# A PSUM source for VectorE's pair differences, and a second of four tiles for GpSimd

## The chip, the cores and the metric

The kernel runs on one core of a Trainium2 chip. A core has TensorE (PE in the profile, with its weight loads as PEld), VectorE (DVE), ScalarE (ACT), GpSimd (POOL), and queues that issue DMAs (SP's above all). The metric is device time of one execution in microseconds (us); lower is better.

## The reference, cut to what matters

Four graph layers, each `x = x + layer(relu(layernorm(x)), adj)`, over 128 graphs of 128 nodes with 128 channels, all in float32. Layer 1 is the one that the change touches:

```python
D = jnp.abs(x[:, :, None, :] - x[:, None, :, :])      # 128 graphs x 128 x 128 pairs x 128 channels
h = jnp.einsum('bijc,oc->bijo', D, W1) + b1           # 64 outputs for each pair
m = jnp.mean(h, axis=(0, 1, 2))                       # a batch norm over all pairs of all graphs
v = jnp.mean((h - m) ** 2, axis=(0, 1, 2))
h = _leaky((h - m) / jnp.sqrt(v + EPS) * g1 + be1)
s = jnp.einsum('bijo,uo->biju', h, W2)[..., 0] + b2[0]   # then mask, softmax, A @ x, Wg, batch norm, Wt
```

Layer 0 sums, for 7 relations r, the neighbours with `adj == r` through a weight of their own, normalizes and adds. Layers 2 and 3 are masked attention.

## The kernel before, in words

The work goes in 32 groups of G = 4 graphs, and in three stages, since each batch norm of layer 1 needs a sum over all graphs first.

Stage one (lines 216 to 311) holds layer 0 and the pairs of layer 1. `layer0(g)` loads a group, normalizes (`pre_norm`, lines 156 to 165: L146 and L148 statistics on DVE, `rsqrt` on POOL at L140 and L141, L153 scale and L164 relu on DVE), transposes (L170 on PE, L171 on ACT), and for each graph builds a mask tile of 7 relations on DVE (L253), multiplies by the relation weights on PE (`ph`, L259), copies to SBUF on ACT (`hw`, L261), multiplies by the masks on PE (`pa`, L265, and the degrees, L268), and adds the parts up on DVE (L274). Then it normalizes the sum `o` (L279 to L285), stores `x`, normalizes again (`hn`, L290) and transposes into `xe` (L294), an SBUF tile with the channels on the partitions and the first 64 of the 128 nodes repeated at the end (L297, on POOL).

`pairs(g)` takes the pairs (i, j) of one graph by distance: 64 distances in four tiles t = 0 to 3, each of 2 halves x 8 distances x 128 nodes = 2048 elements on 128 partitions. For one tile, `pairwise` (lines 177 to 193) does this:

- `d = xe[shifted] - xe` (L185), one instruction with two SBUF inputs, on POOL where t is in `ON_POOL`, else on DVE;
- the absolute value in place on ACT (L187);
- four matmuls with W1 into a PSUM tile of two banks (`hp`, L191).

`pair_stats` then copies `hp` to SBUF on ACT (`hs`, L205), takes its statistics on DVE (L206, L208, L210) and, once a graph, stores `hs` in HBM (L211).

`_weave` (line 39) writes the program so that four steps of `layer0(g + 2)` follow each tile of `pairs(g)`. A scheduler in the compiler then orders each engine's instructions by its own estimates of durations; each engine runs its order strictly from front to back. So in each group the program has a mixed stretch, in which the matmuls of layer 0 alternate with those of some eight tiles, and a plain stretch of the remaining tiles, in which only the two norms at the end of layer 0 and the first norm of the next group's layer 0 go along. Buffers that set the order: three of `d` (the tag "d"), two of `hp` (the PSUM tag "big", 4 of 8 banks), four of the PSUM tag "sm" (the other 4 banks: `pt`, `po`, `ph`, `pa` in stage one, and nearly all small products later), three of `xe`.

Stage two (line 316 to the `behind` loop) reads the stored `hp` back, applies the batch norm and W2, and does layer 1's softmax and sums. Stage three (`group`, line 576) does the end of layer 1 and layers 2 and 3. Both take their PSUM tiles from the tags "sm" and "big".

Of the kernel before, what the change touches and what calls it, by code (L numbers as in the profile page):

```python
# [9 lines left out]
F32 = mybir.dt.float32  # L10
# [6 lines left out]
P = 128  # L17
G = 4
# [7 lines left out]
KH = 32  # L26
KC = 8
ROW = P + 2 * KH
ON_POOL = {1}
AHEAD = 2  # L30
NT = KH // KC

# [26 lines left out]
def tile_gnn_stack(ctx: ExitStack, tc: tile.TileContext, a: dict, out: bass.AP):  # L59
    nc = tc.nc  # L60
# [6 lines left out]
    psum = ctx.enter_context(tc.tile_pool(name="psum", bufs=1, space=bass.MemoryType.PSUM))  # L67
# [2 lines left out]
        return psum.tile([P, 2, 512], F32, tag="big", bufs=2, name=name)  # L70

    def sm(name):
        return psum.tile([P, G, P], F32, tag="sm", bufs=4, name=name)


    ident = const.tile([P, P], F32, name="ident")
# [51 lines left out]
    HT = [dr.tile([P, G, P], F32, tag=f"h{g}", name=f"h{g}") for g in range(NG)]  # L128
# [24 lines left out]
            nc.vector.tensor_scalar(dst[:, k, :], src[:, k, :], mv[:, k, 0:1], rs[:, k:k + 1],  # L153
                                    op0=OP.subtract, op1=OP.mult)

    def pre_norm(pool, src, mv=None, rs=None):

        if mv is None:
            mv = small.tile([P, G, 2], F32, name="lnmv")
            rs = small.tile([P, G], F32, name="lnrs")  # L160
            norm_stats(src, mv, rs)
        h = pool.tile([P, G, P], F32, tag="hn", name="hn")
        norm(h, src, mv, rs)
        nc.vector.tensor_scalar(h, h, 0.0, None, op0=OP.max)  # L164
        return h

    def transpose(dst, src):
        pt = sm("pt")
        for k in range(G):
            nc.tensor.transpose(pt[:, k, :], src[:, k, :], ident)  # L170
        nc.scalar.copy(dst, pt)  # L171
# [2 lines left out]
        return t[:, None, :].to_broadcast([P, G, P])  # L174


    def pairwise(pool, xe, k, t):

        d = pool.tile([P, 2, KC, P], F32, tag="d", bufs=3, name="d")
        x = xe[:, k, 0:P]  # L180
        ahead = xe[:, k, 1 + KC * t:]
        ahead = bass.AP(tensor=ahead.tensor, offset=ahead.offset,
                        ap=[list(ahead.ap[0]), [KH, 2], [1, KC], [1, P]])
        eng = nc.gpsimd if t in ON_POOL else nc.vector
        eng.tensor_tensor(d, ahead, x[:, None, None, :].to_broadcast([P, 2, KC, P]), OP.subtract)  # L185
        d = d.rearrange("p h k i -> p h (k i)")
        nc.scalar.activation(d, d, AF.Abs)  # L187
        hp = big("hp").rearrange("p a b -> p (a b)")
        for c in range(0, KC * P, 512):
            for hh in range(2):  # L190
                nc.tensor.matmul(hp[64 * hh:64 * hh + 64, c:c + 512], w1T, d[:, hh, c:c + 512],  # L191
                                 start=True, stop=True)
        return hp

    hsp = ctx.enter_context(tc.tile_pool(name="hsp", bufs=3))

    def pair_stats(pool, xe, k, b):


        st = small.tile([P, 9, 6], F32, name="st")  # L200
        hs = hsp.tile([P, NT, KC * P], F32, name="hs")
        for t in range(NT):
            yield
            hp = pairwise(pool, xe, k, t)
            nc.scalar.copy(hs[:, t, :], hp)  # L205
            nc.vector.bn_stats(st[:, 2 * t, :], hs[:, t, 0:512])  # L206
            last = t == NT - 1
            nc.vector.bn_stats(st[:, 2 * t + 1, :], hs[:, t, 512:1024 - P * last])  # L208
            if last:
                nc.vector.bn_stats(st[:, 8, :], hs[:, t, 1024 - P:])  # L210
        nc.sync.dma_start(HP[b], hs)  # L211
        nc.vector.bn_aggr(ST1[:, b, 0, :], st.rearrange("p a b -> p (a b)"))
        nc.vector.bn_aggr(ST1[:, b, 1, :], st[:, 8, :])


    with tc.tile_pool(name="c0", bufs=1) as c0, tc.tile_pool(name="p0", bufs=2) as p0:
        relw = load("relw", [P, 7, P], a["rel_w"][1:8].rearrange("r c d -> c r d"), pool=c0)
        selfwT = load("selfwT", [P, P], a["self_wT"], pool=c0)
        selfb = load("selfb", [P, P], _bcast(a["self_b"], P), pool=c0)
        gamma = load("gamma", [P, P], _bcast(a["gamma"], P), pool=c0)  # L220
        beta = load("beta", [P, P], _bcast(a["beta"], P), pool=c0)

        rel = c0.tile([P, 7], F32, name="rel")
        for r in range(7):
            nc.gpsimd.memset(rel[:, r:r + 1], float(r + 1))

        def layer0(g):
            bs = slice(g * G, g * G + G)
            hT = p0.tile([P, G, P], F32, name="hT")
            x = p0.tile([P, G, P], F32, name="x")  # L230
            nc.sync.dma_start(x, a["x"][bs].rearrange("b t c -> t b c"))
            adj = p0.tile([P, G, P], I32, name="adj")
            nc.sync.dma_start(adj, a["adj"][bs].rearrange("b t s -> t b s"))
            yield
            h = pre_norm(p0, x)
            yield
            adjf = p0.tile([P, G, P], F32, name="adjf")
            nc.vector.tensor_copy(adjf, adj)
            nc.gpsimd.tensor_scalar(M8[g], adjf, 0.0, None, op0=OP.is_gt)
            transpose(hT, h)  # L240
            yield
            adjT = p0.tile([P, G, P], F32, name="adjT")
            transpose(adjT, adjf)
            yield
            o = p0.tile([P, G, P], F32, name="o")
            po = sm("po")
            for k in range(G):
                nc.tensor.matmul(po[:, k, :], hT[:, k, :], selfwT, start=True, stop=True)
            nc.vector.tensor_tensor(o, po, over_group(selfb), OP.add)
            yield  # L250
            for k in range(G):
                mask = p0.tile([P, 7, P], F32, name="mask")
                nc.vector.tensor_tensor(mask, adjT[:, None, k, :].to_broadcast([P, 7, P]),  # L253
                                        rel[:, :, None].to_broadcast([P, 7, P]), OP.is_equal)

                for r0, r1 in ((0, 3), (3, 7)):
                    yield
                    ph = sm("ph")
                    nc.tensor.matmul(ph[:, 0:r1 - r0, :], hT[:, k, :], relw[:, r0:r1, :], start=True, stop=True)  # L259
                    hw = p0.tile([P, G, P], F32, name="hw", bufs=2)  # L260
                    nc.scalar.copy(hw[:, 0:r1 - r0, :], ph[:, 0:r1 - r0, :])  # L261
                    yield
                    pa = sm("pa")
                    for r in range(r0, r1):
                        nc.tensor.matmul(pa[:, r - r0, :], mask[:, r, :], hw[:, r - r0, :], start=True, stop=True)  # L265
                    if r0 == 0:
                        for r in range(7):
                            nc.tensor.matmul(pa[:, 3, r:r + 1], mask[:, r, :], ones[:, 0:1], start=True, stop=True)  # L268
                        rdeg = small.tile([P, 7], F32, name="rdeg")
                        nc.vector.tensor_scalar(rdeg, pa[:, 3, 0:7], 1e-6, None, op0=OP.max)  # L270
                        nc.vector.reciprocal(rdeg, rdeg)
                    yield
                    for r in range(r0, r1):
                        nc.vector.scalar_tensor_tensor(o[:, k, :], pa[:, r - r0, :], rdeg[:, r:r + 1],  # L274
                                                       o[:, k, :], op0=OP.mult, op1=OP.add)
            yield
            mv = small.tile([P, G, 2], F32, name="lnmv")
            rs = small.tile([P, G], F32, name="lnrs")
            norm_stats(o, mv, rs)  # L279
            yield  # L280
            norm(o, o, mv, rs)
            nc.vector.tensor_tensor(o, o, over_group(gamma), OP.mult)
            yield
            nc.vector.tensor_tensor(o, o, over_group(beta), OP.add)
            nc.vector.scalar_tensor_tensor(x, o, 0.0, x, op0=OP.max, op1=OP.add)  # L285
            nc.sync.dma_start(X[g], x)
            yield
            norm_stats(x, MV1[:, g], RS1[:, g])
            yield
            h = pre_norm(p0, x, MV1[:, g], RS1[:, g])  # L290
            yield

            xe = p0.tile([P, G, P + 2 * KH], F32, name="xe", bufs=AHEAD + 1)
            transpose(xe[:, :, 0:P], h)  # L294
            nc.sync.dma_start(HT[g], xe[:, :, 0:P])
            yield
            nc.gpsimd.tensor_copy(xe[:, :, P:], xe[:, :, 0:2 * KH])  # L297
            XE[g] = xe

        def pairs(g):  # L300
            xe = XE.pop(g)
            for k in range(G):
                yield from pair_stats(p0, xe, k, g * G + k)


        XE = {}
        for g in range(AHEAD):
            for _ in layer0(g):
                pass
        for g in range(NG):  # L310
            _weave(pairs(g), layer0(g + AHEAD) if g + AHEAD < NG else iter(()), 4)
# [359 lines left out]
```

## Time and profile before

| What | Value |
|---|---|
| median of 3 runs | 5709.03 us (5699.23 to 5712.11) |
| the profiled execution's own time | 5692.13 us |
| its span in the profile | 5690.3 us |
| stage one, of the span | to about 3010 us |
| stage two, of the span | about 3060 to 4400 us |
| stage three, of the span | about 4400 to 5690 us |
| busy in the span | PE 3734.1, DVE 3804.0, ACT 2626.8, POOL 816.0 us |

The profile is one execution. A row of its groups names line, engine, operation, output tile, input tiles and shape, the number of instructions, busy time in us, the mean duration of one in ns, and the idle time ahead of them with what ended it. PE runs at a granted share of its clock, which is given by stretches. The chain of waits follows, from the last instruction back, what released each step. Stage one repeats itself from group to group: the start of POOL's tile comes back every 90.8 us, for group after group.

### The profile page before, as it was taken

Reading aid. Unit: us, or ns where it says so; the run is one execution under the profiler, and the core shown is the slowest. Engines: PE = TensorE matmul, PEld = TensorE weight load, DVE = VectorE, ACT = ScalarE, POOL = GpSimd, SP = SyncE. Lnnn points to the kernel's source line nnn. Section 1 sums busy time; section 2 is a strip of 40 time slices with the busy share of each in tenths; the row PEclk is TensorE's granted clock in tenths of the full one; section 3 lists DMA queues with packets and bytes.
Section 4 is the critical chain, followed back from the end, with each engine's and each line's share of the span. In section 5 each row is a group of like instructions: output and inputs, shape, how many; then the busy total and the mean of one; then the engine's idle time right before and its main releaser. Section 6 shows DMA issues by size and latency. Waiting matters only on the chain.

```text
span 5690.3 us, 49171 instructions
## 1 busy us (share of the span) xinstructions
PE 3734.1 (66%) x17414; PEld 2055.7 (36%) x17414; DVE 3804.0 (67%) x7803; ACT 2626.8 (46%) x2434; POOL 816.0 (14%) x530
## 2 busy tenths in 40 slices
PE   5776767676777767676755555555546666666665
PEld 3332323232333323232312223322325555555554
DVE  6788888888888888888884333333336666665666
ACT  2455555555555555555565454444432222222222
POOL 2222222222222222222220000000000000000000
PEclk8888888888888888888876677667677667666676
DMA  1222222222222222222226666667640000000000
GB/s 48 100 100 104 96 104 96 118 98 102 98 102 113 102 104 96 104 96 109 98 113 270 260 259 253 244 255 272 242 179 14 15 8 15 11 12 15 8 15 10
DMA packets 167251, 634.40 MB, mean 111 GB/s; under 512 B 28512, under 2 KB 113760, under 8 KB 134240
## 3 DMA queue, kind: packets, MB, share of 16 engines
q1 hardware_dynamic: 150112, 622.87, 28.2%
q10 hardware_dynamic: 16896, 8.39, 0.5%
q8 instruction: 140, 2.29, 0.2%
q14 instruction: 103, 0.84, 0.0%
HBM read 324.18 MB, written 307.04 MB: 111 GB/s over the span
## 4 chain that ended last, share of the span: by engine, by line
PE 47%; DVE 28%; DMA 8%; ACT 7%; POOL 6%; issue 3%; SPq 0%; POOLq 0%; ACTq 0%; DVEq 0%
PE hp L191 15%; DVE d L185 6%; DMA rows<-sk 5%; ACT d L187 4%; PE ps L395 4%; PE pa L265 4%; PE ph L259 4%; PE pv L549 4%; PE pa L268 3%; DMA u<-rows 3%; POOL d L185 3%; PE pk L402 3%; PE pt L170 3%; DVE hn L153 2%; DVE st L206 2%
## 5 line engine op out<-in xcount | busy, mean ns | idle before, releaser
L191 PE MATMUL hp<-d,w1T 128*64 128x512 f32 x4096 | 1329.5, 742 | 798.1 <-ACT d L187 798.1
L187 ACT ACTIVATE d<-d 128x2048 f32<-128x2048 f32 x512 | 974.6, 1911 | 430.2 <-POOL d L185 224.6
L185 DVE TENSOR_TENSOR d<-xe 128x2048 f32<-128x2048 f32 x384 | 1099.6, 2863 | 14.0 <-PE hp L191 14.0
L191 PEld LDWEIGHTS hp<-d,w1T 128*64 128x64 f32 x4096 | 329.6, 164 | 1588.7 <-ACT d L187 951.6
L205 ACT COPY hs<-hp 128x1024 f32<-128x1024 f32 x512 | 516.0, 1008 | 515.6 <-PE hp L191 513.3
L185 POOL TENSOR_TENSOR d<-xe 128x2048 f32<-128x2048 f32 x128 | 544.4, 4253 | 1452.7 <-PE hp L191 1452.6
L391 ACT ACTIVATE z<-z,bias,scale 128x2048 f32<-128x2048 f32 x256 | 524.9, 2086 | 267.2 <-DMA z<-hp 267.1
L206 DVE BATCH_NORM_STATS2 st<-hs 128x6 f32<-128x512 f32 x512 | 350.8, 685 | 99.5 <-ACT hs L205 95.1
L170 PE MATMUL pt<-ident,e 128*128 128x128 f32 x768 | 154.9, 352 | 313.9 <-ACT e L533 233.0
L395 PE MATMUL ps<-z,w2z 128*32 128x512 f32 x2048 | 340.2, 782 | 4.7 <-ACT z L391 4.6
L265 PEld LDWEIGHTS pa<-hw,mask 128*128 128x128 f32 x1792 | 238.6, 205 | 252.3 <-issue 144.1
L208 DVE BATCH_NORM_STATS2 st<-hs 128x6 f32<-128x512 f32 (+1 forms) x512 | 329.0, 643 | 0.0
L430 PE MATMUL put<-ident,u 128*128 128x128 f32 x128 | 35.6, 434 | 437.8 <-DVE u L426 437.8
L265 PE MATMUL pa<-hw,mask 128*128 128x128 f32 x1792 | 289.6, 306 | 28.8 <-ACT hw L261 24.0
L261 ACT COPY hw<-ph 128x384 f32<-128x384 f32 (+1 forms) x256 | 136.3, 532 | 365.9 <-PE ph L259 365.2
L170 PE MATMUL pt<-ident,hn 128*128 128x128 f32 x512 | 121.1, 381 | 269.7 <-DVE hn L164 204.3
L274 DVE SCALAR_TENSOR_TENSOR o<-pa,rdeg,o 128x128 f32<-128x128 f32 x896 | 291.5, 337 | 9.4 <-PE pa L265 8.7
L426 DVE TENSOR_TENSOR u<-u 128x256 f32<-128x256 f32 x32 | 13.6, 425 | 393.7 <-DMA u<-rows 393.7
L259 PE MATMUL ph<-relw,hT 128*128 128x384 f32 (+1 forms) x512 | 273.7, 619 | 0.0
L171 ACT COPY hT<-pt 128x512 f32<-128x512 f32 x96 | 56.4, 587 | 444.3 <-PE pt L170 444.3
L140 POOL TENSOR_SCALAR lnrs<-lnmv 128x4 f32<-128x4 f32 x128 | 34.7, 271 | 1567.3 <-DVE lnmv L148 1567.3
L170 PEld LDWEIGHTS pt<-ident,e 128*128 128x128 f32 x768 | 112.6, 179 | 395.5 <-ACT e L533 260.8
(154 smaller groups left out, 5658.1 us busy)
## 6 DMA issues: line engine op xcount, KB each, us to landing
hp<-hs SPq DMA_DIRECT2D x128, 2048.0 KB, 6.3
z<-hp SPq DMA_DIRECT2D x128, 2048.0 KB, 9.8
x<-x SPq DMA_DIRECT2D x128, 256.0 KB, 3.0
u<-rows SPq DMA_DIRECT2D x32, 384.0 KB, 5.6
x<-in_x_dram SPq DMA_DIRECT2D x32, 256.0 KB, 2.7
adj<-in_adj_dram SPq DMA_DIRECT2D x32, 256.0 KB, 2.8
h<-xe SPq DMA_DIRECT2D x32, 256.0 KB, 6.3
hT<-h SPq DMA_DIRECT2D x32, 256.0 KB, 2.6
```

What stands on the lines that cost most here:

```text
L170: nc.tensor.transpose(pt[:, k, :], src[:, k, :], ident)
L185: eng.tensor_tensor(d, ahead, x[:, None, None, :].to_broadcast([P, 2, KC, P]), OP.subtract)
L187: nc.scalar.activation(d, d, AF.Abs)
L191: nc.tensor.matmul(hp[64 * hh:64 * hh + 64, c:c + 512], w1T, d[:, hh, c:c + 512], start=True, stop=True)
L205: nc.scalar.copy(hs[:, t, :], hp)
L206: nc.vector.bn_stats(st[:, 2 * t, :], hs[:, t, 0:512])
L208: nc.vector.bn_stats(st[:, 2 * t + 1, :], hs[:, t, 512:1024 - P * last])
L259: nc.tensor.matmul(ph[:, 0:r1 - r0, :], hT[:, k, :], relw[:, r0:r1, :], start=True, stop=True)
L265: nc.tensor.matmul(pa[:, r - r0, :], mask[:, r, :], hw[:, r - r0, :], start=True, stop=True)
L274: nc.vector.scalar_tensor_tensor(o[:, k, :], pa[:, r - r0, :], rdeg[:, r:r + 1], o[:, k, :], op0=OP.mult, op1=OP.add)
L391: nc.scalar.activation(zn, zn, AF.Prelu, bias=bias1, scale=scale1[:, 0:1], alpha=0.01)
L395: nc.tensor.matmul(ps[q:q + 32, :], w2z[:, w:w + 32], zn[:, 512 * c:512 * c + 512], start=j < 4, stop=j >= 4, skip_group_check=True)
```

## The change

Four things, all in stage one but for the bank.

- `ON_POOL` goes from {1} to {1, 3}: POOL computes tiles 1 and 3 of each graph, DVE tiles 0 and 2.
- The transposed group stays in a PSUM bank of its own (`xp`) while its pairs are computed. For a DVE tile, the operand that is the same for all distances is read from `xp`; the shifted one still comes from `xe` in SBUF. POOL's tiles read `xe` twice, as before.
- The bank is taken from the tag "sm", which has three buffers instead of four, in all stages. `d` gets two buffers for DVE's tiles and two for POOL's, instead of three for both.
- The transposes into `xp`, the copy to `xe` and the copy of the 64 repeated nodes (now a second ACT instruction, not a POOL one) move from the end of `layer0` to the head of `pairs`; `layer0` leaves the normalized group (`h1`, three buffers) behind. `xe` has two buffers.

```diff
-ON_POOL = {1}
+ON_POOL = {1, 3}
...
-        return psum.tile([P, G, P], F32, tag="sm", bufs=4, name=name)
+        return psum.tile([P, G, P], F32, tag="sm", bufs=3, name=name)
...
-    def pairwise(pool, xe, k, t):
+    def pairwise(pool, xe, xp, k, t):
...
-        d = pool.tile([P, 2, KC, P], F32, tag="d", bufs=3, name="d")
-        x = xe[:, k, 0:P]
+        on_pool = t in ON_POOL
+        d = pool.tile([P, 2, KC, P], F32, tag=f"d{int(on_pool)}", bufs=2, name="d")
+        x = (xe if on_pool else xp)[:, k, 0:P]
...
-        eng = nc.gpsimd if t in ON_POOL else nc.vector
+        eng = nc.gpsimd if on_pool else nc.vector
         eng.tensor_tensor(d, ahead, x[:, None, None, :].to_broadcast([P, 2, KC, P]), OP.subtract)
...
-            h = pre_norm(p0, x, MV1[:, g], RS1[:, g])
-            yield
-
-            xe = p0.tile([P, G, P + 2 * KH], F32, name="xe", bufs=AHEAD + 1)
-            transpose(xe[:, :, 0:P], h)
+            H1[g] = pre_norm(p0, x, MV1[:, g], RS1[:, g], tag="h1", bufs=AHEAD + 1)
+
+        def pairs(g):
+
+            h = H1.pop(g)
+            xp = psum.tile([P, G, P], F32, tag="xp", name="xp")
+            for k in range(G):
+                nc.tensor.transpose(xp[:, k, :], h[:, k, :], ident)
+            xe = p0.tile([P, G, P + 2 * KH], F32, name="xe")
+            nc.scalar.copy(xe[:, :, 0:P], xp)
+            nc.scalar.copy(xe[:, :, P:], xp[:, :, 0:2 * KH])
             nc.sync.dma_start(HT[g], xe[:, :, 0:P])
-            yield
-            nc.gpsimd.tensor_copy(xe[:, :, P:], xe[:, :, 0:2 * KH])
-            XE[g] = xe
-
-        def pairs(g):
-            xe = XE.pop(g)
-            for k in range(G):
-                yield from pair_stats(p0, xe, k, g * G + k)
+            for k in range(G):
+                yield from pair_stats(p0, xe, xp, k, g * G + k)
```

More of the change, by code (lines that the diff above doesn't have):

```diff
@@ L154, in norm, with pre_norm @@
                                     op0=OP.subtract, op1=OP.mult)
-    def pre_norm(pool, src, mv=None, rs=None):
+    def pre_norm(pool, src, mv=None, rs=None, tag="hn", bufs=2):
         if mv is None:
@@ L161, in pre_norm @@
             norm_stats(src, mv, rs)
-        h = pool.tile([P, G, P], F32, tag="hn", name="hn")
+        h = pool.tile([P, G, P], F32, tag=tag, bufs=bufs, name="hn")
         norm(h, src, mv, rs)
@@ L195, in tile_gnn_stack, with pair_stats @@
     hsp = ctx.enter_context(tc.tile_pool(name="hsp", bufs=3))
-    def pair_stats(pool, xe, k, b):
+    def pair_stats(pool, xe, xp, k, b):
         st = small.tile([P, 9, 6], F32, name="st")
@@ L203, in pair_stats @@
             yield
-            hp = pairwise(pool, xe, k, t)
+            hp = pairwise(pool, xe, xp, k, t)
             nc.scalar.copy(hs[:, t, :], hp)
@@ L289, in layer0 @@
             yield
-            h = pre_norm(p0, x, MV1[:, g], RS1[:, g])
-            yield
-            xe = p0.tile([P, G, P + 2 * KH], F32, name="xe", bufs=AHEAD + 1)
-            transpose(xe[:, :, 0:P], h)
-            nc.sync.dma_start(HT[g], xe[:, :, 0:P])
-            yield
-            nc.gpsimd.tensor_copy(xe[:, :, P:], xe[:, :, 0:2 * KH])
-            XE[g] = xe
-        def pairs(g):
-            xe = XE.pop(g)
+            H1[g] = pre_norm(p0, x, MV1[:, g], RS1[:, g], tag="h1", bufs=AHEAD + 1)
[7 more added lines that the diff above has]
+            nc.scalar.copy(xe[:, :, P:], xp[:, :, 0:2 * KH])
+            nc.sync.dma_start(HT[g], xe[:, :, 0:P])
             for k in range(G):
-                yield from pair_stats(p0, xe, k, g * G + k)
-        XE = {}
+                yield from pair_stats(p0, xe, xp, k, g * G + k)
+        H1 = {}
         for g in range(AHEAD):
```

## The prediction

> **What bounds the kernel now.** I read the page first: which engines are busy, and where.
>
> ```profile
> PE 3734.1 (66%) x17414; PEld 2055.7 (36%) x17414; DVE 3804.0 (67%) x7803; ACT 2626.8 (46%) x2434; POOL 816.0 (14%) x530
> ...
> DVE  6788888888888888888884333333336666665666
> ...
> L185 DVE TENSOR_TENSOR d<-xe 128x2048 f32<-128x2048 f32 x384 | 1099.6, 2863 | 14.0 <-PE hp L191 14.0
> ...
> L185 POOL TENSOR_TENSOR d<-xe 128x2048 f32<-128x2048 f32 x128 | 544.4, 4253 | 1452.7 <-PE hp L191 1452.6
> ```
>
> DVE is eight tenths busy through stage one and idles little; POOL stands idle. That invites the change, but a share is an average. So next the query of all d on DVE, of norms (L153) early in the run, and the timeline there:
>
> ```profile
> L185 DVE TENSOR_TENSOR d<-xe x384: 2245/2281/5934, 75.5 to 3007.6; 128x2048 f32<-128x2048 f32 x192
> ```
> ```profile
> L153 DVE TENSOR_SCALAR hn<-x,lnmv,lnrs x4: 333/368/4326, 70.0 to 74.8; 128x128 f32<-128x128 f32 x4
> ```
> ```profile
> 69.99 5.16 DVE L153 TENSOR_SCALAR hn<-x,lnmv,lnrs 128x128 f32<-128x128 f32 x4 [1.48 <-POOL lnrs L141]
> ...
> 70.39 4.17 POOL L185 TENSOR_TENSOR d<-xe 128x2048 f32<-128x2048 f32 x1
> ```
>
> The columns are min/median/max in ns; start and length in us. A d on DVE takes 2.28 us, but up to 5.93, mean 2.86: it is held while POOL computes a d. The norm shows the same: one of four small instructions takes 4.33 us instead of 0.33, just the length of POOL's d beside it, which had come straight behind another POOL instruction. POOL won.
>
> Last, one period of 90.7 us cut in two, the plain stretch (from the last `pa` to the next `po`) and the mixed one, and two groups at the end that have no layer 0:
>
> ```profile
> 1590.00:1635.20 45.20, 41.10 (x192) 20.93 (x192) 36.29 (x69) 24.87 (x24) 5.59 (x3) 0.92 0.22 94
> 1635.20:1680.70 45.50, 23.71 (x84) 7.44 (x84) 40.16 (x72) 25.96 (x20) 16.03 (x11) 0.77 0.29 115
> 2892.40:2994.90 102.50, 59.66 (x192) 16.51 (x192) 94.02 (x85) 67.68 (x49) 25.09 (x7) 0.80 0.29 123
> ```
>
> After the length stand the busy us of PE, PEld, DVE, ACT, POOL. The mixed stretch belongs to PE (41.1 of 45.2), the plain one to DVE (40.2 of 45.5), the end to DVE (94.0 of 102.5).
>
> [...] d and L153 above are held; L274, which takes one input from PSUM, never passes 0.352 us in 896, though POOL's d cover 544 us.
> [...] 128x512 takes 0.668 us from PSUM and SBUF (L249), 0.692 from SBUF alone (L282). I take 0[...]. No reason makes it a gain.
> [...] the trace's 4.19 (median) is used.
>
> **The parts.**
> *Work taken off DVE.* 128 d of 2.863 us = 366 us leave. The other 256 are no longer held: 256 x (2.863 - 2.281) = 149. Together 515 us of DVE's busy time. That is not the gain: it counts only where DVE sets the end.
> *Work given to POOL.* 128 x 4.25 = 544 us, on an engine idle 86%. Who waits: ACT's absolute value behind each, and in ACT's strict order all that stands after it. In the changed program's order, three POOL tiles of the mixed stretch have ACT waiting for POOL with an `hw` copy behind it, which PE's `pa` waits for: by the rows about 1.4 to 2.4 us each. Fewer waits for DVE balance this. Mixed stretch: 45 us, as before.
> *Copies and transposes.* The transposes move, their 0.66 us per group remains; POOL's 0.40 us copy becomes ACT's 0.40. The HT store moves too on SP's queue; its data are read a stage later. Nothing.
> *Three "sm" banks.* In stages two and three the order on each engine is the same as before. Laying the new banks over the times of the profiled execution, no tile finds its bank taken; the narrowest margin is 0.4 us. That margin is the cover; without it 0.4 us per tile would be at stake. I take 0.
> *The last two groups.* Eight graphs at 17.07 us (the stretch above, 102.5 by 6), bound by DVE. Then ACT: four absolute values of 1.82 and four copies of 0.9 (spacing in the timeline) is 10.9 us; with waits I take 12, so 8 x 5 = 40 us gained.
> *The plain stretch, 30 times.* Here the moved steps count. I walk the changed order by hand with durations of the rows, from the end of the last matmul of the mixed stretch:
> - DVE ends its sums and statistics at 4.0, then two d, to 8.5. Norm of `o`, gamma, beta, residual, statistics: 4.45 us by the rows, to 12.95. Its next d: 15.2.
> - POOL's rsqrt needs those statistics: to 14.4. Right behind, POOL's order has d (tile 1), 14.4 to 18.6, and d (tile 3), ready since 16: to 22.8. In DVE's order, the four `hn` norms come next at 15.2: held to 22.8, **7.6 us**. Behind them are queued four tiles' statistics and DVE's last d of the group.
> - Norms 1.1, relu 0.35, statistics 4.85, d 2.25: 31.4. ACT's absolute value and both copies of `xe`, which has to follow: 34.2.
> - POOL's first d of the next group: 38.4; rsqrt: 39.7; its second d directly: 44.0. DVE's norms wait for that rsqrt and are held by that d, **4.3 us**: 45.1. A d, statistics, relu: 49.1. Transposes, ACT's copy, PE's remaining three matmuls: `po` can start at 51.7. With 0.5 us from the last `pa`: 52.2 against 45.5.
>
> [...] before, POOL had one d in the plain stretch's way, never right behind an rsqrt.
> *Sum.* The plain stretch grows by 6.7, the mixed one loses 0.2 to 1; say +6.0 a group. 30 x 6.0 = 180, less 40, is **+140 us**. Against the profiled execution (5692.1, its span 5690.3 and 1.8 around it) that is 5832. The median of the runs is 17 higher, 5709, so I say 5849.
>
> **The rivals.**
> *DVE gets its turn (faster).* If the norms slip in between POOL's d, the plain stretch loses up to 7.6 + 4.3 = 11.9 us: 30 x (6.0 - 11.9) - 40 = -217, 5492. Place: the norms after the two rsqrt. For it: only one norm in the trace is shown held. Against it: POOL won there, when both stood ready. It decides below a hold of 7.2 us a group (where 30 x (hold - 5.9) = 40). A hold of 6 to 2 us gives 5672 to 5552; so would a walk that overstates waits elsewhere.
> *PE is held more (slower still).* If ACT's waits for POOL in the mixed stretch aren't paid for by fewer waits for DVE, three of some 2 us add 5 a group: +150, 5999. For it: PE has only 4 us idle there. Against it: DVE's d wait for nothing there now.
> *DVE's busy time is the gain.* 5709 - 515 = 5194. Against it: PE's 41 of 45 us in half of the period.
> *The change doesn't do what it says,* d is held despite PSUM: L274 speaks against it; with twice the POOL time, up to twice 1.8 us for each that meets, it would end slower than forecast.
>
> **How the numbers follow.** Forecast (hold as walked, 5760 to 5950): 0.52. Slower still: 0.17. DVE gets its turn, in whole or part: 0.25. Within 0.2%: 0.05, between the two. Busy-time gain: 0.01. 0.2% is about what a measurement of this kernel can tell from no change. So faster 0.26, same 0.05, slower 0.69. The forecast's own range is 5760 to 5950; the range from 5560 to 5990 takes in most of the rival on the fast side, the likelier half of the slow one[...].
>
> **What would show it.** d on DVE at 2.28 with no tail to 5.9; L153 `hn` with a tail of 4 to 8 us and its mean well over 0.34; mask tiles (L253 before) with some at 4; a period near 97 us; POOL busy about 1,350; the last graphs near 12 us each; stages two and three as long as before (2,630 us). I am wrong if the norms stay at 0.34, if PE fills the plain stretch, or if stages two and three move.

## The result, and the profile after

| | before | after |
|---|---|---|
| median of 4 runs each, same chip | 5707.96 us | 5996.59 us (5990.84 to 6005.31) |
| ratio | | 1.051, interval 1.049 to 1.053 |
| span of the profiled execution | 5690.3 us | 5990.0 us |

The change costs 289 us where I had forecast a loss of 140. I read the trace after in the order in which I had read the one before. First the busy times, then the groups (line, operation, tile and shape, count; busy us and mean ns; idle us ahead of it and what ended the idle time):

```profile
PE 3844.9 (64%) x17414; PEld 2136.0 (36%) x17414; DVE 3662.3 (61%) x7675; ACT 2629.5 (44%) x2466; POOL 1322.8 (22%) x626
```
```profile
L188 POOL TENSOR_TENSOR d<-xe 128x2048 f32<-128x2048 f32 x256 | 1069.7, 4185 | 1573.2 <-PE hp L194 1240.8 <-ACT xe L303 331.7
L190 ACT ACTIVATE d<-d 128x2048 f32<-128x2048 f32 x512 | 976.8, 1914 | 651.6 <-POOL d L188 451.8 <-DVE d L188 196.0
L188 DVE TENSOR_TENSOR d<-xe,xp 128x2048 f32<-128x2048 f32 x256 | 579.5, 2264 | 10.9 <-PE hp L194 10.8
L268 PE MATMUL pa<-hw,mask 128*128 128x128 f32 x1792 | 301.4, 314 | 187.0 <-ACT hw L264 187.0
```

The change does what it says: d on DVE has a mean of 2.264 us, where it was 2.863, and none passes 2.289, where the longest took 5.934; POOL does twice as many d. Two waits in these rows have grown. ACT's absolute value waits 452 us for POOL (225 before), and PE's `pa` waits 187 us for `hw` (24 before; both rows of before stand below). A row of waits says who stood still, not yet at whose cost.

```profile
L187 ACT ACTIVATE d<-d 128x2048 f32<-128x2048 f32 x512 | 974.6, 1911 | 430.2 <-POOL d L185 224.6 <-DVE d L185 203.9
...
L265 PE MATMUL pa<-hw,mask 128*128 128x128 f32 x1792 | 289.6, 306 | 28.8 <-ACT hw L261 24.0 <-DVE mask L253 4.8
```

Then the norms, as min/median/max in ns. The tail that I had forecast is there:

```profile
L153 DVE TENSOR_SCALAR hn<-x,lnmv,lnrs x384: 323/340/4201, 21.7 to 5962.1; 128x128 f32<-128x128 f32 x192
L153 DVE TENSOR_SCALAR hn<-x,MV,RS x256: 332/342/4248, 70.6 to 4513.0; 128x128 f32<-128x128 f32 x128
```

The chain of waits through one plain stretch shows where (start us, length us, what):

```profile
1318.86 2.25 DVE d L188
1321.11 8.23 DVE hn L153 x4
...
1334.49 2.20 DVE d L188
...
1339.56 4.19 POOL d L188
...
1345.10 4.96 DVE hn L153 x4
...
1359.47 0.45 PE po L251
```

Four norms of 0.34 us each take 8.23 us in one place and 4.96 in the other, so they are held for 6.9 and 3.6 us. The walk of the prediction had these two places, with 7.6 and 4.3 us.

Last, one period in its two stretches (after the length: busy us of PE, PEld, DVE, ACT, POOL with their numbers of instructions, then PE's granted clock; the last two columns, of the DMAs, are not used):

```profile
1254.40:1305.40 51.00, 44.82 (x192) 24.30 (x192) 25.16 (x59) 20.07 (x20) 12.55 (x3) 0.83 0.10 42
1305.40:1359.40 54.00, 27.33 (x86) 8.52 (x87) 48.68 (x76) 31.09 (x24) 26.10 (x12) 0.72 0.34 136
```

As means over 24 groups in the middle of stage one, the period is 104.1 us where it was 92.2. (The 90.8 us named ahead of the prediction hold for some groups only: before, the starts of POOL's tiles lie 89.4 to 94.9 us apart from group to group.) The mixed stretch has grown from 46.5 to 50.3 us (+3.8), the plain one from 45.7 to 53.8 (+8.1). Up to the second of these periods, stage one takes 16 us more. From there to the last `pa` it takes 331 more, which is 28 times 11.8. From there to the end of stage one it takes 49 less, and stages two and three take 2 more: 16 + 331 - 49 + 2 = 300, as much as the spans differ by.

### The profile page after: what moved, and what is told of

Its sections match the earlier page's. It is cut to its first block, busy times and chain, and to the rows that moved or that the text cites. A ratio compares the mean times of both kernels' runs of the same rounds, so it can differ in the third digit from the quotient of the medians.

```text
span 5990.0 us, 49292 instructions
## 1 busy us (share of the span) xinstructions
PE 3844.9 (64%) x17414; PEld 2136.0 (36%) x17414; DVE 3662.3 (61%) x7675; ACT 2629.5 (44%) x2466; POOL 1322.8 (22%) x626
## 4 chain that ended last, share of the span: by engine, by line
PE 42%; DVE 32%; POOL 9%; DMA 8%; ACT 4%; issue 4%; SPq 0%; POOLq 0%; ACTq 0%; DVEq 0%
PE hp L194 10%; DVE hn L153 8%; POOL d L188 7%; DVE d L188 5%; DMA rows<-sk 5%; PE pa L271 4%; PE ps L398 4%; PE ph L262 4%; PE pa L268 4%; PE pv L552 3%; PE pt L170 3%; DMA u<-rows 3%; PE pk L405 2%; DVE st L209 2%; POOL lnrs L141 2%
## 5 line engine op out<-in xcount | busy, mean ns | idle before, releaser
L188 POOL TENSOR_TENSOR d<-xe 128x2048 f32<-128x2048 f32 x256 | 1069.7, 4185 | 1573.2 <-PE hp L194 1240.8
L188 DVE TENSOR_TENSOR d<-xe,xp 128x2048 f32<-128x2048 f32 x256 | 579.5, 2264 | 10.9 <-PE hp L194 10.8
L170 PE MATMUL pt<-ident,hn 128*128 128x128 f32 x384 | 105.2, 429 | 377.6 <-DVE hn L164 313.4
L273 DVE TENSOR_SCALAR rdeg<-pa 128x7 f32<-128x7 f32 x128 | 21.2, 166 | 485.0 <-PE pa L271 485.0
L262 PE MATMUL ph<-relw,hT 128*128 128x384 f32 (+1 forms) x512 | 309.3, 692 | 0.6 <-DVE rdeg L274 0.6
L153 DVE TENSOR_SCALAR hn<-x,MV,RS 128x128 f32<-128x128 f32 x256 | 284.2, 1171 | 19.0 <-DMA x<-x 10.6
L153 DVE TENSOR_SCALAR hn<-x,lnmv,lnrs 128x128 f32<-128x128 f32 x384 | 218.9, 633 | 96.1 <-POOL lnrs L141 96.1
```

## The experiments

Each ratio to the kernel before has an interval of some 0.1 to 0.4% either way. In the table, period and stretches are means over the same 24 groups, and "held" is the time per group by which DVE's instructions exceed the median of their kind (same operation, tiles and shape, over all these kernels), where they exceed it by more than 0.1 us. "Fixed" means the order of instructions, of which more below.

| kernel | time us | ratio | period | mixed | plain | held |
|---|---|---|---|---|---|---|
| before | 5708 | 1 | 92.2 | 46.5 | 45.7 | 6.9 |
| after | 5997 | 1.051 | 104.1 | 50.3 | 53.8 | 12.4 |
| PSUM operand alone | 5611 | 0.983 | 88.7 | 52.9 | 35.8 | 4.8 |
| second POOL tile alone | 5987 | 1.049 | 102.1 | 54.6 | 47.6 | 7.4 |
| before, norms on ACT | 5705 | 1.000 | 92.1 | 47.0 | 45.2 | 8.5 |
| after, norms on ACT | 5408 | 0.948 | 82.6 | 43.0 | 39.7 | 7.3 |
| after, hw on DVE | 5643 | 0.989 | 90.5 | 47.8 | 42.7 | 3.6 |
| after, norms on ACT and hw on DVE | 5748 | 1.007 | 95.5 | 59.0 | 36.5 | 12.3 |
| after, three POOL buffers | 5885 | 1.030 | 99.3 | 48.5 | 50.8 | 16.1 |
| after, norms in steps of two | 5990 | 1.050 | 104.1 | 50.3 | 53.8 | 12.4 |
| after, POOL waits for norms, fixed | 5977 | 1.048 | 103.2 | 52.5 | 50.7 | 2.9 |
| after, hw on DVE, fixed | 5806 | 1.018 | 97.4 | 43.5 | 53.9 | 11.3 |
| after, both of these, fixed | 5778 | 1.013 | 96.4 | 45.7 | 50.7 | 2.0 |
| after, three POOL buffers, fixed | 5608 | 0.983 | 90.5 | 36.9 | 53.5 | 12.4 |
| after, three DVE buffers, fixed | 5997 | 1.051 | 104.1 | 50.3 | 53.8 | 12.4 |
| three POOL buffers and POOL waits, fixed | 5564 | 0.975 | 89.0 | 38.3 | 50.7 | 4.1 |
| before, four d buffers, fixed | 5581 | 0.978 | 88.8 | 44.8 | 43.9 | 5.1 |
| norms on ACT, three POOL buffers | 5571 | 0.977 | 88.9 | 45.6 | 43.2 | 5.1 |
| the same, fixed | 5242 | 0.919 | 77.9 | 40.3 | 37.6 | 8.1 |

### Which half of the change costs

Theory 1 was that of the prediction: with POOL's second d, holds like that of the norm that took 4.33 us instead of 0.33 fall on the norms of every group. Theory 2 was its rival: ACT waits for POOL's d, in its strict order holds `hw` behind it, and so PE. The first runs take the change apart.

The PSUM operand alone:

```diff
-ON_POOL = {1, 3}
+ON_POOL = {1}
```

> The changed kernel with POOL at tile 1 alone: xp in PSUM, three sm banks, moved transposes and ACT copies all stay. Theory 1 (POOL's second d[...] holds the norms, +8.1 us in the plain stretch) and theory 2 (ACT waits for POOL's d in its strict order and holds hw and so PE, +3.8 us in the mixed stretch) both need the second POOL tile: here the period comes down to 92 us or below, norms at 0.34 us with almost no tail, time 5550 to 5710 us (up to 6 us a group less than before, since no d is held any more). Rival: the PSUM operand, the third bank or the moved steps are what costs: then most of the +289 stays and the time is over 5850 us.

Measured: 5611 us, and the norm behind MV has no tail (335/342/349 ns). The PSUM operand by itself, with xp, three banks and moved steps, gains 99 us. That is 3.5 us a group, less than the 6.9 us of holds that it lifts from d. Part of the hold has moved to the mask tiles, whose mean goes from 1.11 to 2.17 us, and PE's `pa` now waits for them:

```profile
L256 DVE TENSOR_TENSOR mask<-adjT,rel 128x896 f32<-128x896 f32 x128 | 277.6, 2170 | 28.3 <-PE pa L268 26.8 <-ACT adjT L171 1.4
L268 PE MATMUL pa<-hw,mask 128*128 128x128 f32 x1792 | 295.7, 306 | 149.1 <-DVE mask L256 113.6 <-ACT hw L264 34.2
```

The second POOL tile alone, in the kernel before:

```diff
-ON_POOL = {1}
+ON_POOL = {1, 3}
...
-        d = pool.tile([P, 2, KC, P], F32, tag="d", bufs=3, name="d")
+        d = pool.tile([P, 2, KC, P], F32, tag=f"d{int(t in ON_POOL)}", bufs=2, name="d")
```

> The kernel before with POOL at tiles 1 and 3 (d in two tags of two buffers), without xp, with four sm banks and the old place of the transposes. Theories 1 and 2: all of the cost is here, and d on DVE is held on top: 5980 to 6200 us, norms with a tail of 4 us, d on DVE with a tail to 6 us. Rival (PSUM operand, banks or moved steps cost): 5700 to 5850 us.

Measured: 5987 us, 279 over the kernel before. So the loss comes with the second POOL tile, and beside it the PSUM operand is worth nothing (5987 without, 5997 with it). In both runs the scheduler chose an order of its own: 8.0 of a group's 16 tiles lie in the mixed stretch with the PSUM operand alone, 6.8 with the second POOL tile alone, 7.0 before and 6.9 after. What the two parts are worth under one and the same order is not shown.

Three "sm" banks in the kernel before:

```diff
-        return psum.tile([P, G, P], F32, tag="sm", bufs=4, name=name)
+        return psum.tile([P, G, P], F32, tag="sm", bufs=3, name=name)
```

> The kernel before with three sm banks instead of four in all stages, nothing else. As predicted (no tile finds its bank taken): 5700 to 5715 us, within 0.2%. Rival (the narrow margin of 0.4 us does not hold): 0.4 us at a good part of the tiles, 5730 to 5800 us.

Measured: 5716 us, ratio 1.001, interval 1.000 to 1.002. The bank costs at most 0.2%.

### First trials of the two theories

Norms and relu ahead of both transposes on ACT, in the changed kernel and, as a control, in the one before (POOL works out `nb`, the bias -mean/sigma, around its rsqrt; the cut below is the one of the changed kernel):

```diff
+    def act_norm(h, src, rs, nb):
+        for k in range(G):
+            nc.scalar.activation(h[:, k, :], src[:, k, :], AF.Relu, bias=nb[:, k:k + 1], scale=rs[:, k:k + 1])
...
-            h = pre_norm(p0, x)
...
+            act_norm(h, x, rs, nb)
...
-            H1[g] = pre_norm(p0, x, MV1[:, g], RS1[:, g], tag="h1", bufs=AHEAD + 1)
...
+            act_norm(H1[g], x, RS1[:, g], nb)
```

> The changed kernel with the norms and relu ahead of both transposes of stage one done by ACT (one activation for each graph: scale 1/sigma, bias -mean/sigma, which POOL computes right behind its rsqrt), so that no norm of hn can be held on DVE. Theory 1: the plain stretch gives back about 8 us, 30 x 8 = 240: 5700 to 5800 us; theory 2's +3.8 us in the mixed stretch stays. Rival: the norms were late because rsqrt stood late in POOL's queue[...]: no more than 60 us gained, 5930 to 6000 us.

> The kernel before with the hn norms and relu of stage one on ACT. It is the control for the same edit on the changed kernel. Theory 1: before, no norm was held to speak of, so only their own 3.4 us of DVE work a group leave the plain stretch: at most 30 x 3.4 = 102 us, 5600 to 5710 us, a gain of well under half of what the same edit gives on the changed kernel. Rival: the edit gains by itself, whatever POOL does: 200 us or more here too.

Then `hw` copied by DVE (the first diff), both edits together, and a third buffer for POOL (the second):

```diff
-                    nc.scalar.copy(hw[:, 0:r1 - r0, :], ph[:, 0:r1 - r0, :])
+                    nc.vector.tensor_copy(hw[:, 0:r1 - r0, :], ph[:, 0:r1 - r0, :])
```
```diff
-        d = pool.tile([P, 2, KC, P], F32, tag=f"d{int(on_pool)}", bufs=2, name="d")
+        d = pool.tile([P, 2, KC, P], F32, tag=f"d{int(on_pool)}", bufs=2 + on_pool, name="d")
```

> The changed kernel with the copies of ph to hw on DVE, so that they no longer stand behind ACT's absolute values that wait for POOL. Theory 2: PE's wait for hw (11 us in one mixed stretch, 3 before) goes, the mixed stretch comes back to 46 to 47 us though DVE gets 4.5 us of copies: 5870 to 5920 us. Rival (PE's lower granted clock, 0.83 to 0.86 against 0.89 to 0.92, is the cause of the longer mixed stretch, not the result of waits): mixed stretch stays at 50 us or more, 5980 to 6100 us.

> The changed kernel with both edits: hn norms on ACT and hw copies on DVE. Theories 1 and 2 together: 5996 - 240 - 100 = 5650 us (5600 to 5720), period near 92 to 94 us, so the change's cost is gone. Rival (ACT's or DVE's new work becomes the bound): 5750 us or more.

> The changed kernel with three d buffers for POOL instead of two (DVE keeps two). Theories 1 and 2: POOL's d come no later for want of a buffer[...]: 5970 to 6020 us. Rival: POOL starts its d late because both its buffers are taken (its idle time is put down to PE's hp), so that a third lets it run ahead and ACT wait less: 30 x 2 to 4 us less, 5880 to 5940 us.

Measured: norms on ACT 5408 us (gaining 589, where theory 1 gave 200 to 300), the control 5705 (nothing), `hw` on DVE 5643 (354, where theory 2 gave about 100), both together 5748, the third buffer 5885 (112, as its rival said). Each alone seems to bear out its theory, and too well; together they are worse than either. The table hints at the reason. Held time differs from kernel to kernel, and so does the number of a group's 16 tiles that lie in the mixed stretch (6.9 after, 7.9 with norms on ACT, 7.9 with three buffers; an expectation further down says that two tiles moved with the buffer, and it is one). With each edit the compiler's scheduler had put the engines' instructions in a new order. These five runs are therefore inconclusive on the causes.

### Norms in steps of two

One way to keep the order is to alter only how an instruction reads and writes (the relu behind the norm is altered likewise):

```diff
+swap = lambda t: t.rearrange("p (a b) -> p b a", b=2)
...
-            nc.vector.tensor_scalar(dst[:, k, :], src[:, k, :], mv[:, k, 0:1], rs[:, k:k + 1],
+            nc.vector.tensor_scalar(swap(dst[:, k, :]), swap(src[:, k, :]), mv[:, k, 0:1], rs[:, k:k + 1],
```

> The changed kernel with one thing altered: VectorE's norms (L153) and the relu behind them (L164) read and write their elements in steps of two (even ones, then odd ones), the same elements with the same values. Every engine's order of instructions stays that of the changed kernel, which it did not in the earlier edits. Theory 1[...]: norms at 0.35 to 0.45 us with no tail to 4 us, the plain stretch shorter by 6 to 11 us of its 53.8, 5996 - 30 x 6 to 11 = 5670 to 5820 us. The mixed stretch stays near 50 us. Rival (norms are long because their data or the semaphore of rsqrt come late[...]): tail stays at 4 us and the time at 5980 to 6020 us.

Measured: 5990 us, and durations as they were:

```profile
L153 DVE TENSOR_SCALAR hn<-x,MV,RS x256: 333/343/4232, 65.9 to 4522.7; 128x128 f32<-128x128 f32 x128
```

The median is 0.343 us and the longest 4.23, where they were 0.342 and 4.25 in steps of one. The norms are held as before, so the run tells nothing of what the holds cost. That an access in steps of two would keep the tail away was an estimate of mine that no trace had shown.

### The order fixed

Edges between neighbours of one engine's order that carry no wait (NoSync) hold the scheduler to an order taken from another kernel. With the changed kernel's own order of stage one put in like this (in short; the edges are all that is added), every engine runs its instructions in the same order as without, and the time is the same: 5997 us, in the run further down that also gives DVE a buffer that it does not need.

```python
for names in ORDER:                                # one list for each engine
    for a, b in zip(names, names[1:]):
        tc.add_manual_dep(tc.nc.get_inst_by_name(b), a, nosync, reason="order")
```

Under that order I took away the hold by letting POOL give way instead: an added wait (`sync`) of POOL's d for the relu behind the norm, from the norms of the sixth group on. `DS` lists POOL's d, eight for each group, and `RELU` the relu of each norm, two for each group:

```diff
+    for q in range(3, 32 - AHEAD):
+        tc.add_manual_dep(DS[8 * q + 6], RELU[2 * (q + AHEAD) + 1].name, sync, reason="norm first")
+        if q + AHEAD + 1 < 32:
+            tc.add_manual_dep(DS[8 * q + 9], RELU[2 * (q + AHEAD + 1)].name, sync, reason="norm first")
```

> The changed kernel with every engine's order in stage one fixed to that of the changed kernel, and one added wait: in each group POOL's first d behind the rsqrt of the last norm, and its d behind the rsqrt of the next group's first norm, wait until VectorE has written the norm and its relu. Nothing is left out; POOL gives way instead of DVE. Theory 1[...]: the 11 us of holds a group go to nearly 0 at the price of some 2 us by which POOL's d start later, the plain stretch falls from 53.8 to 44 to 47 us, the mixed one stays at 50: 5996 - 30 x 7 to 10 = 5700 to 5790 us. Rival (the norms' wait hides behind other work, ACT and PE wait for POOL's d anyway): the period stays over 101 us, 5900 us or more.

Then `hw` on DVE alone, both, and the third POOL buffer alone, all under that order:

> The changed kernel with the copies of ph to hw on DVE, and the order of PE, POOL and the rest of ACT and DVE in stage one fixed to that of the changed kernel; only the hw copies are put in. In the first trial of this edit the order of all engines had changed with it. Theory 2 (ACT waits in its order for POOL's d and hw and PE wait behind it): the mixed stretch falls from 50.3 to 46.5 to 48 us, the plain one stays at 53 to 54: 5996 - 30 x 2.3 to 3.8 = 5880 to 5930 us. Rival (the gain of the first trial came from the new order alone; hw on DVE waits as long): mixed stretch 50 us or more, 5980 us or more.

> The changed kernel with both: POOL's d wait for the norms, and hw copies on DVE; order fixed as in the two runs by themselves. Theories 1 and 2 as two causes that add: 5996 - 30 x (7 to 10) - 30 x (2.3 to 3.8) = 5590 to 5720 us, at or below the kernel before. Rival (one of them covers the other, ACT or DVE takes over): no more than 20 us below the better of the two by themselves.

> The changed kernel with three d buffers for POOL, the order of every engine in stage one fixed to that of the changed kernel. If the 112 us that the free order gained with this edit came from the buffer (POOL runs ahead and ACT waits less): 5860 to 5920 us again. If they came from the order that the compiler's scheduler then chose (two tiles a group moved into the mixed stretch): 5970 to 6010 us.

Measured: with POOL giving way 5977 us; with `hw` on DVE 5806; with both 5778, between its two ranges; with a third POOL buffer 5608, far below both of its ranges. Theory 1 falls as an account of the size: the held time goes from 12.4 to 2.9 us a group, and the time falls by 19 us. (What the holds would be worth without a later d of POOL's, this run doesn't show; norms on ACT under the fixed order were not tried with two buffers.) Theory 2 stands, and gives more than I had put on it (191 us), though PE's `pa` still waits 140 us, now for the copies on DVE. And the buffer, which neither theory had, gives 389 us with every hold still in place. Its windows, same columns, same instructions in the same order:

```profile
1300.60:1337.30 36.70, 36.70 (x192) 19.67 (x191) 25.45 (x60) 20.07 (x20) 17.09 (x4) 1.00 0.14 58
1337.30:1391.20 53.90, 27.73 (x87) 8.62 (x86) 48.64 (x76) 31.10 (x24) 23.37 (x12) 0.72 0.34 137
```

The plain stretch has not moved (53.9). The mixed one falls from 51.0 to 36.7 us, PE is busy in all of it, and its clock is 1.00 instead of 0.83. In the rows of this run, ACT's wait for POOL has all but gone, 62 us where it was 452 (its wait for DVE rose from 196 to 296), and with it PE's wait for `hw`, 8.5 us where it was 187:

```profile
L188 POOL TENSOR_TENSOR d<-xe 128x2048 f32<-128x2048 f32 x256 | 1099.5, 4301 | 866.9 <-PE hp L194 530.4 <-ACT xe L303 336.3
L190 ACT ACTIVATE d<-d 128x2048 f32<-128x2048 f32 x512 | 980.5, 1917 | 358.2 <-DVE d L188 296.1 <-POOL d L188 62.0
L268 PE MATMUL pa<-hw,mask 128*128 128x128 f32 x1792 | 274.2, 294 | 8.5 <-ACT hw L264 8.5
```

### The loop in the mixed stretch

With this in hand I went back to the changed kernel's timeline (start us, length us, then in brackets the idle time ahead and its releaser):

```profile
1273.50 4.19 POOL L188 TENSOR_TENSOR d<-xe 128x2048 f32<-128x2048 f32 x1 [7.82 <-PE hp L194]
...
1277.72 1.91 ACT L190 ACTIVATE d<-d 128x2048 f32<-128x2048 f32 x1 [3.32 <-POOL d L188]
1279.54 0.46 ACT L264 COPY hw<-ph 128x384 f32<-128x384 f32 x1
...
1280.05 0.94 PE L268 MATMUL pa<-hw,mask 128*128 128x128 f32 x6 [3.09 <-ACT hw L264]
...
1280.83 2.62 PE L271 MATMUL pa<-ones,mask 128*128 128x1 f32 x14
```

POOL's d stands 7.82 us until PE's `hp` of an earlier tile gives one of POOL's two buffers free, and then takes 4.19. ACT has come to this tile's absolute value and stands idle for 3.32 us, though the `ph` that its next `hw` copy reads was done at 1275.10. The `hw` copy behind it in ACT's order is late, PE's `pa` waits 3.09 us for it, and in PE's order the next `hp`, which would free POOL's next buffer, stands behind `pa`. So the loop runs: POOL's buffer, PE, ACT, POOL. I call this theory 3. Two things open the loop: a buffer more (5608 us), or, in part, `hw` off ACT's queue (5806). With POOL's added wait, which makes its d later, the mixed stretch grows to 52.5 us, as the loop would have it.

PE's standing still is the smaller part of the cost. The same stretch, cut at PE's two waits:

```profile
1268.00:1276.80 8.80, 8.80 (x48) 4.54 (x45) 7.17 (x17) 4.32 (x5) 3.30 (x1) 1.00 0.22 91
1276.80:1280.10 3.30, 0.21 (x3) 0.05 (x1) 0.75 (x4) 2.38 (x3) 0.89 (x1) 1.00 0.93 397
1280.10:1288.60 8.50, 8.50 (x31) 4.55 (x31) 3.51 (x9) 3.21 (x3) 0.00 (x0) 0.60 0.00 0
1288.60:1295.20 6.60, 3.58 (x18) 1.58 (x18) 2.69 (x8) 3.27 (x4) 4.19 (x1) 0.98 0.01 1
1295.20:1303.50 8.30, 8.23 (x27) 5.11 (x27) 2.79 (x11) 1.52 (x3) 0.00 (x0) 0.50 0.00 1
```

After each of the two waits PE runs its next 8 us at a mean clock of 0.60 or 0.50. The two waits are 3.1 and 3.0 us; by an estimate from these lines, the slow clock costs 8.5 x 0.40 + 8.3 x 0.50 = 7.6 us. Together that is 13.7 us, against 13.4 between the mean mixed stretches with two and with three buffers. The two windows of whole stretches bear it out: the same 192 matmuls keep PE busy for 44.82 us here and for 36.70 with three buffers (8.1 us more), and PE stands still for 6.2 us here and not at all there. That the clock falls with the waits, and not the waits with the clock, is seen from the buffer: it takes away the waits, and the clock is at 1.00.

For most of each of these two stretches the clock stands at one value: it is 0.50 from 1281.3 to 1288.0 us and from 1294.9 to 1305.1. PE was busy for 6.7 and 9.8 us of these two spans before the clock came back, to 0.96 in the 0.6 us behind the first and 0.99 in the 0.9 us behind the second. What sets these lengths is not shown.

### Which buffer, and what the hold is worth without the loop

The fifth buffer to DVE instead of POOL (`bufs=3 - on_pool`), and a fourth one for the kernel before (`bufs=4`), each in its own kernel's order:

> The changed kernel with the fifth d buffer given to DVE instead of POOL (DVE three, POOL two), order fixed. Theory 3 (POOL's own buffer closes the loop; DVE's d waits for a buffer 11 us in the whole run): nothing changes, 5970 to 6010 us, mixed stretch near 50 us. Rival (any further buffer loosens the stage, as the fourth one did for the kernel before): 5600 to 5850 us.

> The kernel before with four d buffers instead of three, order of every engine in stage one fixed to that of the kernel before. It is the control for the buffer. Theory 3: before, POOL has one d a graph and no more than 1 us of ACT's wait for it falls in a mixed stretch, so the loop hardly closes: 5650 to 5710 us. Rival: a fourth buffer would have done as much for the kernel before: 5400 to 5600 us.

Measured: 5997 us, no change at all, for DVE's buffer. It is POOL's buffer that counts. And 5581 us for the kernel before with four shared buffers, 127 us less than with three. Theory 3 had given it 5650 us at least; 5581 lies in the range of the rival, so the kernel before was short of a buffer too. There the gain is not that of the loop alone: the mixed stretch falls by 1.7 us, at a clock of 0.92 as before, and the plain one by 1.8, with 1.8 us less of holds. Which of these is the cause there stays open. With one buffer more in each, the changed kernel is 27 us behind (5608 against 5581). So 389 - 127 = 262 of the 289 us go with the buffers, each kernel in its own order.

Then both, three POOL buffers and POOL's added wait:

> The changed kernel with three d buffers for POOL and also the added wait of POOL for the two norms, order fixed. Theory 3 (formed from the last four runs: with two buffers POOL's d waits for PE's hp, which stands behind pa, which waits for hw, which stands in ACT's order behind the absolute value of that very d; the clock of PE falls with its waits): with the third buffer the mixed stretch is bound by PE at full clock, so that what the norms' hold costs in the plain stretch is no longer hidden: 53.5 falls to 46 to 50 us, 5608 - 30 x 3 to 7 = 5400 to 5520 us. Rival: POOL's waiting costs what the holds cost: 5590 to 5630 us.

Measured: 5564 us, 44 less than with the buffer alone and between the two ranges. Of the holds, 8.3 us a group are gone, yet the plain stretch falls by only 2.8 us. Its chain of waits shows why:

```profile
1327.28 1.03 DVE hn L153 x4
...
1329.40 0.26 POOL d L188
1329.66 3.89 issue
1333.55 4.20 POOL d L188
1337.78 1.56 ACT d L190
...
1343.22 4.19 POOL d L188
...
1353.81 4.18 POOL d L188
```

The norms take 1.03 us again, and in their place stand POOL's four d, 4.2 us each (the first shows as 0.26 and 3.89). Two POOL tiles a graph make POOL itself part of the plain stretch's path. Of the 8.3 us that DVE no longer stands still, the period gets 1.5. ACT's absolute value now waits 286 us for POOL's d where it was 62 with the buffer alone, and 123 for DVE's where it was 296.

### A kernel that beats both

Norms on ACT leave no `hn` of stage one on DVE to be held (other holds remain: in the faster run below `o`'s norms have a mean of 1.19 us, where it was 0.34 after, and the masks one of 2.17, where it was 1.39), and three buffers open the loop:

> The changed kernel with norms on ACT and three d buffers for POOL, order left to the scheduler. If both gains add as far as the bounds allow (PE's 37 us at full clock in the mixed stretch, DVE's some 37 in the plain one): period 74 to 80 us, 5150 to 5350 us. If the order that the scheduler picks is a poor one again: 5400 us or more.

> The same two edits with the order of every engine in stage one fixed to that of the run with norms on ACT and two POOL buffers (5408 us). Theory 3: the third buffer gains here too, though less than the 389 us, since ACT's waits for POOL there were 277 us in all: 5200 to 5350 us. Rival: the loop was broken there already, 5390 to 5420 us.

Measured: 5571 us with the scheduler's order, 5242 with the order of the run with norms on ACT (ratio 0.919, interval 0.916 to 0.921). The second lies in the range of theory 3. The two differ in nothing but the order, by 329 us. How much of the gain over 5608 us is that of the norms and how much that of the order, no run separates. Mixed, plain and the next mixed stretch of the faster:

```profile
1059.70:1100.30 40.60, 39.92 (x200) 20.91 (x200) 34.67 (x66) 28.30 (x26) 23.30 (x6) 0.96 0.20 85
1100.30:1133.70 33.40, 20.93 (x77) 6.18 (x76) 29.71 (x60) 25.41 (x29) 18.35 (x14) 0.85 0.45 180
1133.70:1173.00 39.30, 38.47 (x200) 20.33 (x200) 35.97 (x67) 28.44 (x26) 23.28 (x6) 1.00 0.21 89
```

PE is busy in 38 to 40 of 39 to 41 us of the mixed stretch, at 0.96 to 1.00.

## Why the prediction was right and wrong, point by point

- **DVE's and POOL's work.** DVE's busy time fell by 142 us. Its d alone gave back 520 (515 forecast), but holds of 12.4 us a group came on norms (11.0) and mask tiles. It was right that this sum isn't the gain. POOL's rose by 507 (544 given).
- **PSUM source at nothing.** Right: 2.264 us, against 2.281 from SBUF, the median before.
- **Three "sm" banks, copies and transposes at nothing.** The banks right within 0.2%. Copies and transposes weren't tried alone; with the PSUM operand, and in an order of the scheduler's own, they gained 99 us together.
- **The last two groups.** From the first to the last `hp` of the eight graphs it was 130.7 us before and is 89.7 after: 41 us gained, 40 forecast, at 11.2 us for each graph (12 forecast). Right.
- **The plain stretch.** The walk held: 11.0 us of holds on the norms (11.9 walked), at the two places named, +8.1 us (+6.7). That POOL wins when it stands right behind its own rsqrt was right at both: its d start at 1320.41 and 1345.04 us, the norms at 1321.03 and 1345.10. At the first, of four norms DVE got one through between two d. What the walk couldn't tell is what the hold is worth: taken away by letting POOL wait, it gave 19 us (44 with three buffers), since POOL's d then stand on the path themselves.
- **The mixed stretch "45 us, as before".** This is the step that failed. "Fewer waits for DVE balance this" didn't come: ACT's wait for DVE was 204 us before and is 196 after, while its wait for POOL doubled, and 46.5 us went to 50.3. It failed in three parts. First, I never costed the split of the d buffers, two for POOL, as a wait: I read the new tags as a detail of the change. A third buffer takes 389 us off. Second, I priced PE's waits at their own length, three of 1.4 to 2.4 us. The two in the stretch shown, 3.1 and 3.0 us, are within that sum, but the slow clock behind them more than doubled it. Third, I read "PE 41.1 of 45.2" as PE at its bound: the same 192 matmuls run in 36.7 us once nothing makes them wait.
- **The rivals.** "PE is held more", at 0.17, is what happened, by the mechanism given (ACT's waits for POOL in its strict order, `hw` behind them), and its 5999 us stands beside 5997 measured. That is closer than it deserves: it had +5 a group on +6.7 in the plain stretch, and measured are +3.8 on +8.1, with 49 us less at the end. The two numbers met by luck.
- **The sum.** 30 x 6.0 - 40 = 140 against 28 x 11.8 + 16 - 49 + 2 = 299 in the spans: what is missing is 4 to 5 us a group in the mixed stretch, 1.4 in the plain one, and 16 at the start.
- **The signs of being wrong.** None of the three came: the norms did not stay at 0.34 us, PE did not fill the plain stretch (27 of 54 us), stages two and three moved by no more than 2 us. Only the period, 104 us where 97 was forecast, gave the miss away. No sign watched the mixed stretch, which was taken as it was, and there the forecast failed.

What stays open: which order the scheduler will choose for an edit, and so what the edit is worth with it. The orders here differ by up to 329 us for one and the same work, and no view of the profile before told them. The kernels before and after have different orders too, and no run gave both the same one. So what part of the loss belongs to the order is not shown, nor what makes the 27 us that remain between the two kernels with a buffer more each.

## What to carry to other kernels

When a step moves to a slower engine (a d takes 2.26 us on DVE, 4.19 on POOL), count its buffers as carefully as its time: ask which instruction gives the buffer back, what stands ahead of that in its engine's order, and whether the chain comes back to the step itself. Price a wait of PE with the clock behind it (two waits of 6.1 us in all had slow stretches behind them that cost 7.6 us more, by the estimate above), and don't take PE's busy share at a clock under 1.00 for its bound (the same 192 matmuls kept PE busy for 44.82 us at a mean clock of 0.83 and for 36.70 at 1.00). And where a scheduler picks the order, fix the order before an experiment is believed: with the order free, norms on ACT seemed to prove a theory by 589 us; with the order held, letting POOL give way to the norms was worth 19.

## What the runs showed of the hardware that I had not expected

- PE's granted clock changed within one stretch: 1.00 ahead of a wait of 3.1 us, 0.60 over the 8.5 us behind it, 0.50 over 8.3 us behind the next. A group of 14 one-column matmuls takes 1.62 us at 1.00 and 2.62 in the first of these two stretches.
- A `tensor_scalar` of 128x128 float32 read and written in steps of two takes 0.343 us, as in steps of one (0.342), and is held as long (4.23 us at most, 4.25 in steps of one).
- Behind two d of POOL's in a row (8.34 us), DVE gets through one of four waiting norms between them: the first takes 3.66 us, the second 4.22, and the last two 0.33 each.
